# A graph-attention layer whose projection uses seven half-height products per pair, and one early sum made by VectorE

## The chip, the core and the metric

The kernel runs on one core of a Trainium2 chip. A core has TensorE (PE, with its weight loads shown apart as PEld), VectorE (DVE), ScalarE (ACT), GpSimd (POOL) and SyncE (SP), each with its own instruction queue; semaphores order them against each other. Data lie in SBUF, matmul results in PSUM, which has eight banks of 128 x 512 float32. The metric is the device time of one execution in microseconds. The kernel before took 1846.09 us, the median of three runs (1845.35, 1846.09, 1849.65).

## What is computed

Two layers over a graph of 4096 nodes with 512 float32 features each. Each layer normalizes its input, takes the positive part, and adds the layer's output to the input.

```python
# layer 0: a graph convolution with the dense matrix
rowsum = adj.sum(axis=1)
d = where(rowsum > 0, rowsum ** (-0.5), 0.0)
x = x + relu((d[:, None] * adj * d[None, :]) @ h @ W0 + b)      # h = relu(layernorm(x))
# layer 1: attention over the entries of adj that are above 0
e = leaky_relu(Wh1 + Wh2.T, 0.2)                                # Wh = h @ W, times two halves of a
p = softmax(where(adj > 0, e, -1e12), axis=1)
n = -softmax(where(adj > 0, -e, -1e12), axis=1)
x = x + elu(concatenate([p @ h, n @ h], axis=1) @ wtrans)       # wtrans is 1024 x 512
```

About 0.8% of the matrix is above 0 (an entry is drawn with 1/256, then made symmetric), so layer 1 needs only few rows of h for each block of nodes.

## The kernel before, in words

**Layer 0** (to about 960 us) is a dense product in which blocks of the matrix are added on VectorE before they are multiplied (L1105). Meanwhile it finds, for every 128 rows, which columns occur, and writes the new h, with the attention scores and a mask of bytes, to tables in DRAM.

**Layer 1** works on blocks of 64 nodes; two blocks are a pair, which owns 128 rows of the output. A pair's needed rows of h are fetched by 21 indirect DMAs on GpSimd (`gather`, L506; 8, 6 and 7 of them for the parts a = 0, 1, 2), each bringing 128 rows, and one plain load on SP (`load_own`) for the pair's own rows. Every part has two buffers (`g_pools[k % 2, a]`), used in turn. An even block uses parts 0 and 1 (15 slots of 128 rows), an odd one parts 1 and 2 (14 slots).

For a block r there are these steps:

- `weights(r)` (L1756-1791), for each of the two parts: ScalarE copies the gathered scores into a PSUM bank (e, L1765), VectorE adds the block's own scores (z, L527), ScalarE scales (L1768), VectorE takes the maximum (L1769), ScalarE forms exp of z and of -z (L1773), VectorE masks both into p (L1777). At the end one VectorE reduction over the slots gives the sums (`total`, L1787). z and e take a PSUM bank each.
- `product(r)`: one matmul of `total` with ones (cs, L580), then the matmuls of p with the gathered rows (u, L556). Here p has 64 columns a slot, 32 nodes times two signs, and the two halves of a block stand side by side on TensorE, in columns 0-63 and 64-127. VectorE inverts the sums (L585, L588) and ScalarE scales u (us, L1815).
- `turn(r)`: four transposes of us on TensorE (tp, L595) and two ScalarE copies (ut, L602), one for each sign, into the pair's `uts`.
- The pair's projection: `project1(j, 0)` and `project1(j, 1)`, four matmuls of 128 x 512 each (L1826) into one bank; the second is part of `finish1`, which then applies elu, adds x1 and stores (L1843-1848). The profile counts two passes for a float32 matmul, so a half is eight instructions there.

The order on each engine is written out by the loop over `order`, 62 blocks: at step k come product(k); the gathers for the pair two ahead, part 0 at even k, parts 1 and 2 at odd k; weights(k + 2); turn(k - 1); then the first half of a projection at odd k, or finish1 at even k. Queues are in order, so an instruction that waits holds up what stands behind it on its engine. A gather waits until the last matmul that reads its buffer is done. PSUM banks are given out in turn from one pool of eight (`bank`), so a new tile waits for the tile eight allocations before it.

The last pair is treated apart (`finish_last`, L1856-1873, two column halves of 256, matmuls L1860).

**The early pair.** Pair 16, blocks 33 and then 32, is done inside the end of layer 0, because layer 0 leaves its last two tiles of h (`late_h`) for the end: `early_pair` (L1496) gathers its rows ahead, makes weights and products while layer 0 finishes, and adds the late rows (`late_weights0`, `late_product0`) when they exist. Its sums are matmuls with one column: one for every slot, 14 for block 33 and 15 for block 32 (`sum0`, L1541), and then the late ones, which end the same accumulation.

Of the kernel before, what the change touches and what calls it, by code (L numbers as in the profile page):

```python
# [273 lines left out]
def gcn_gat_kernel(  # L274
# [54 lines left out]
    ps = ctx.enter_context(tc.tile_pool(name="ps", bufs=8, space=PSUM))  # L329
    dram = ctx.enter_context(tc.tile_pool(name="dram", bufs=1, space=DRAM))  # L330

    def bank(name):
        return ps.tile([P, 512], F32, tag="ps", name=name)
# [257 lines left out]
    def turn_u(r, u, ut, pin=False):  # L591

        tp = ps.tile([P, FC, 2, 2, SB], F32, tag="ps", name=f"tp{r}")
        for c in range(FC):
            i = nc.tensor.transpose(  # L595
                tp[:, c].rearrange("p h g i -> p (h g i)"), u[:, c * P : (c + 1) * P], ident
            )
# [7 lines left out]
    late_mask = ctx.enter_context(sbuf(name="late_mask", bufs=1, side="right"))  # L605
    late_m = late_mask.tile([P, EJ, TT * P], U8, name="late_m")
    with sbuf(name="y0", bufs=1) as y_pool, sbuf(name="wa", bufs=1) as wa_pool, sbuf(name="bits", bufs=4) as bits_pool, sbuf(name="small0", bufs=4) as small, ExitStack() as rest, ExitStack() as lists:
# [104 lines left out]
        def sum_counts(g):  # L712
            o_ps = places[g] = ps.tile([NH, NE + 1, NK + 1], F32, tag="ps", name=f"o_ps{g}")
# [782 lines left out]
        def early_pair(work, at_pool, prod, rows):  # L1496

            late = ctx.enter_context(sbuf(name="late", bufs=1, side="right"))
# [38 lines left out]
            def sum0(r, ks):  # L1537
                if r not in sums0:
                    sums0[r] = bank(f"cs{r}")
                for k in ks:  # L1540
                    nc.tensor.matmul(  # L1541
                        sums0[r][:, 0:1],
                        ps0[r][:, k].rearrange("p h g i -> p (h g i)"),
                        ones[:, 0:1],
                        start=k == 0,
                        stop=k + 1 == slots0(r) + n_late,
                    )

# [63 lines left out]
            mask0(first)  # L1612
            product0(first)
# [13 lines left out]
            for r in (first, second):  # L1627
                sum0(r, range(slots0(r)))
# [62 lines left out]
    def sparse_layer1():  # L1691
        nonlocal verdict
        with ExitStack() as pools:
# [60 lines left out]
            def weights(r):  # L1754
# [6 lines left out]
                for gt, k, n in parts(r):  # L1761
# [3 lines left out]
                    nc.scalar.copy(e[:, :, 0:1], t)  # L1765
                    scores(s, z, e[:, :, 0:1])
# [50 lines left out]
            def turn(r):  # L1817
                if r % 2 == 0:
                    uts[r // 2] = ut_pool.tile([P, 2, FC, P], F32, tag="ut", name=f"ut{r // 2}")
                turn_u(r, us.pop(r), uts[r // 2])  # L1820
# [14 lines left out]

            def finish1(j):
                x1 = work.tile([P, F], F32, tag="x1", name=f"x1_{j}")
                nc.sync.dma_start(out=x1, in_=x1_dram[j])
                project1(j, 1)
                del uts[j]  # L1840
                po = halves.pop(j)
# [3 lines left out]
                y = work.tile([P, F], F32, tag="y", name=f"y1_{j}", bufs=1)  # L1845
# [4 lines left out]

            def finish_last(j):

                e = work.tile([P, F], F32, tag="eo", name=f"eo{j}", bufs=1)
                y = work.tile([P, F], F32, tag="y", name=f"y1_{j}", bufs=1)
                for h in range(2):
                    cols = slice(h * H, (h + 1) * H)  # L1856
                    po = bank(f"o1_{j}_{h}")[:, :H]
                    for g in range(2):
                        for c in range(FC):
# [3 lines left out]
                                wts[g][:, c, cols],  # L1863
# [7 lines left out]
                    nc.vector.scalar_tensor_tensor(yh, po, 0.0, last_x1[:, cols], ALU.max, ALU.add)  # L1871
# [7 lines left out]
            lates, halves = {}, {}  # L1879
# [23 lines left out]
            for k, r in enumerate(order):  # L1903
# [11 lines left out]
                if k + 2 < len(order):  # L1915
                    weights(order[k + 2])
                    if wanted and order[k + 2] % 8 == 7:
                        load_s(wanted.pop(0))
                if k:
                    turn(order[k - 1])  # L1920
# [13 lines left out]
                if k % 2 and k > 1:  # L1934
                    project1(order[k - 3] // 2, 0)
                elif k > 2:
                    finish1(order[k - 4] // 2)
            last_x1 = work.tile([P, F], F32, tag="x1", name="x1_last")
            nc.sync.dma_start(out=last_x1, in_=x1_dram[order[-1] // 2])
# [45 lines left out]
```

## Time and profile before

| what | us |
|---|---|
| median of three runs | 1846.09 |
| the profiled execution | 1844.97 |
| its span, first to last instruction | 1843.2 |
| PE / DVE / ACT / POOL busy | 1825.7 / 1332.2 / 674.4 / 821.7 |
| u products, L556, 2604 instructions | 572.4 |
| projections, L1826, 496 instructions | 223.2 |
| sums over slots, L1787, 62 instructions | 209.1 |
| gathers of layer 1, L506, 672 instructions | 637.5 |
| early sums, L1541, 66 matmuls from 982.6 to 997.0 | 250 ns median each |

Times of instructions on TensorE overlap: matmuls are pipelined, and a following one starts before the last has drained, so the mean of an instruction is longer than the distance from one to the next. For what a group costs, the distance between starts, or a stretch of the chain of waits, is read. GpSimd's busy time covers the work on a DMA's descriptors, not the transfer, and what lies between two gathers shows as idle time. In a row of the costliest groups the columns are busy time, mean duration in ns of one, and the idle time before them with what ended it. In a row of stretches the columns are the stretch, its length, the busy times (with counts) of PE, PEld, DVE, ACT and POOL, then the granted TensorE clock, the share of the DMA engines and GB/s.

### The profile page before, as it was taken

How to read it: one execution, taken by the hardware profiler on the slowest of the kernel's cores; microseconds unless marked ns; L12 is line 12 of the kernel's file. 1: busy time of each engine (PE TensorE's matmuls, PEld its weight loads, DVE VectorE, ACT ScalarE, POOL GpSimd, SP SyncE). 2: the span in 40 equal slices, each digit the busy share in tenths (PEclk: the TensorE clock that was granted, in tenths of full speed). 3: DMA queues.
4: the chain of work that ended last, by engine and by line, in shares of the span. 5: the costliest groups of instructions: out<-in, count | busy, mean ns of one | idle time of the engine just before them, and what ended most of it. 6: DMA issues, size and time to landing. Idle time of an engine off the chain costs nothing.

```text
span 1843.2 us, 23672 instructions
## 1 busy us (share of the span) xinstructions
PE 1825.7 (99%) x7708; PEld 1035.6 (56%) x7708; DVE 1332.2 (72%) x2882; ACT 674.4 (37%) x1390; POOL 821.7 (45%) x919
## 2 busy tenths in 40 slices
PE   8999999999999999999999999999999999999998
PEld 3444448888888888888744333333333333333333
DVE  6766669799988999897536777677666767676671
ACT  6777762322122412122223333333333333333331
POOL 3101000003432132433067777777777777777740
PEclk9999999999999999999999999999999999999999
DMA  9999975848684859494799999999899988988860
GB/s 370 402 335 333 338 250 184 276 143 280 193 276 151 271 176 289 139 285 148 230 329 350 318 303 311 335 310 343 287 350 301 331 296 298 303 288 289 297 208 25
DMA packets 217212, 504.28 MB, mean 274 GB/s; under 512 B 35059, under 2 KB 69395, under 8 KB 217078
## 3 DMA queue, kind: packets, MB, share of 16 engines
q0 software_dynamic: 62560, 233.71, 37.6%
q1 hardware_dynamic: 108864, 225.92, 36.1%
q10 hardware_dynamic: 45654, 43.04, 7.3%
q8 instruction: 63, 1.03, 0.2%
q14 instruction: 71, 0.58, 0.1%
HBM read 457.77 MB, written 103.45 MB: 304 GB/s over the span
## 4 chain that ended last, share of the span: by engine, by line
PE 96%; DMA 2%; DVE 1%; issue 0%; ACT 0%; ACTq 0%; DVEq 0%; SPq 0%
PE p L1105 33%; PE u L556 32%; PE o L1826 12%; PE acc L1064 5%; PE yp L890 5%; PE q L1465 3%; PE tp L595 2%; DMA ar<-in_adj 2%; PE counts L867 1%; PE tx L831 1%; PE cs L1541 0%; PE cs L580 0%; PE o L1860 0%; DVE key L429 0%; DVE lst L427 0%; DMA w_sb<-in_w 0%
## 5 line engine op out<-in xcount | busy, mean ns | idle before, releaser
L506 POOL DMA_INDIRECT g<-table,idx x672 | 637.5, 949 | 277.9 <-issue 172.1
L556 PE MATMUL u<-g,p 128*64 128x512 f32 x2604 | 572.4, 595 | 0.0
L556 PEld LDWEIGHTS u<-g,p 128*64 128x64 f32 x2604 | 181.6, 137 | 338.8 <-issue 318.7
L442 POOL DMA_INDIRECT ld<-lst,off x160 | 144.5, 903 | 339.4 <-DMA ld<-lst,off 148.8
L1105 PE MATMUL p<-y,at 128*128 128x256 f32 x832 | 248.0, 380 | 0.0
L1105 PE MATMUL p<-y,sums 128*128 128x256 f32 x832 | 247.4, 379 | 0.0
L1105 PE MATMUL p<-t,sums 128*128 128x256 f32 x832 | 245.3, 379 | 0.0
L1826 PE MATMUL o<-wt,ut 128*128 128x512 f32 x496 | 223.2, 593 | 0.0
L1787 DVE TENSOR_REDUCE total<-p 128x128 f32<-128x1920 f32 (+1 forms) x62 | 209.1, 3372 | 2.0
L1105 PEld LDWEIGHTS p<-t,sums 128*128 128x128 f32 x832 | 158.1, 190 | 21.6 <-issue 0.2
L1105 PEld LDWEIGHTS p<-y,at 128*128 128x128 f32 x832 | 157.2, 190 | 23.1 <-issue 2.2
L1105 PEld LDWEIGHTS p<-y,sums 128*128 128x128 f32 x832 | 158.1, 190 | 21.4
L527 DVE TENSOR_TENSOR z<-e,s 128x512 f32<-128x512 f32 (+1 forms) x112 | 71.3, 637 | 102.4 <-ACT e L1765 102.4
L1826 PEld LDWEIGHTS o<-wt,ut 128*128 128x128 f32 x496 | 89.5, 190 | 89.6 <-issue 89.4
L852 ACT ACTIVATE junk<-ar 128x1024 bf16<-128x1024 f32 x128 | 134.6, 1051 | 8.1 <-DMA ar<-in_adj 5.7
L930 ACT ACTIVATE m<-at 128x1024 uint8<-128x1024 f32 x110 | 113.0, 1047 | 51.9 <-DVE t_all L1032 16.1
L1105 PE MATMUL p<-t,at 128*128 128x256 f32 x416 | 123.9, 380 | 1.2 <-DVE w L975 1.2
L890 PE MATMUL yp<-w_sb,hx_t 128*128 128x512 f32 x256 | 119.0, 609 | 1.2 <-DVE hx_t L836 1.2
L1064 PE MATMUL acc<-y,at 128*128 128x512 f32 x256 | 120.2, 594 | 0.0
L427 DVE MAX8 lst<-key 128x8 f32<-128x488 f32 (+13 forms) x154 | 95.0, 617 | 3.4
L1765 ACT COPY e<-g 128x8 f32<-128x8 f32 (+1 forms) x124 | 22.2, 181 | 203.2 <-DMA g<-table,idx 199.3
L1777 DVE SCALAR_TENSOR_TENSOR p<-g,e 128x512 f32<-128x512 uint8 (+1 forms) x124 | 78.9, 637 | 23.2 <-ACT e L1773 20.1
(221 smaller groups left out, 2006.9 us busy)
## 6 DMA issues: line engine op xcount, KB each, us to landing
ar<-in_adj SPq DMA_DIRECT2D x128, 512.0 KB, 6.9
at<-in_adj_t SPq DMA_DIRECT2D x112, 512.0 KB, 4.8
table<-table SPq DMA_DIRECT2D x45, 1032.0 KB, 8.5
table<-m ACTq DMA_DIRECT2D x48, 256.0 KB, 8.9
g<-table,idx POOLq DMA_INDIRECT x672, 5.0
g<-table SPq DMA_DIRECT2D x32, 322.0 KB, 4.8
at<-in_adj_t SPq DMA_DIRECT2D x32, 256.0 KB, 6.7
xr<-in_x SPq DMA_DIRECT2D x32, 256.0 KB, 5.0
```

Source lines behind the costliest of these rows:

```text
L427: nc.vector.max(top, key)
L442: return nc.gpsimd.indirect_dma_start(out=lst_dram[g][e % TURNS][:, :], out_offset=bass.IndirectOffsetOnAxis(ap=off[g][:, e, c : c + 1], a ...
L506: i = nc.gpsimd.indirect_dma_start(out=gt[:, k, :], out_offset=None, in_=table[2 * n // RPT], in_offset=bass.IndirectOffsetOnAxis(ap=idx[n ...
L556: i = nc.tensor.matmul(u[h * RB : (h + 1) * RB], p[:, k, h].rearrange("p g i -> p (g i)"), row(k), start=begin and k == HALVES[r % 2][h][0 ...
L852: nc.scalar.activation(junk, ar, AF.Identity, accum_out=parts[j][:, c : c + 1])
L890: nc.tensor.matmul(yp, hx_t[j][:, c * P : (c + 1) * P], w0_sb[:, c, :], start=c == 0, stop=c == FC - 1,)
L930: nc.scalar.activation(m, at, AF.Sign)
L1064: nc.tensor.matmul(a, at[:, 0, it * P : (it + 1) * P], y0[j], start=j == 0, stop=j == NJ - 1)
L1105: i = nc.tensor.matmul(out, left[:, x * P : (x + 1) * P], right, start=jp == 0 and first, stop=jp == NP - 1 and (final or not first),)
L1777: nc.vector.scalar_tensor_tensor(p[:, k : k + n, :, g], mask.rearrange(four, h=2), 0.0, x.rearrange(four, h=2), ALU.is_gt, ALU.mult,)
L1787: nc.vector.tensor_reduce(total, q, AX.X, ALU.add)
L1826: i = nc.tensor.matmul(halves[j], uts[j][:, g, c, :], wts[g][:, c, :], start=g == 0 and c == 0, stop=g == 1 and c == FC - 1,)
```

## The change

It has two parts.

The early pair: after block 33's masks, one VectorE reduction over its 14 slots puts the sums into a corner of `ut0` (`sum_first`), and one matmul with ones takes the place of the 14 (`begin_sum`). Block 32 keeps its 15.

Layer 1's projection, for the pairs 2 to 29 of the 31 in `order`, becomes a product of 2 x 2 blocks by seven products instead of eight. The left matrix of a pair has 64-row blocks a11, a21 (the positive sign, even and odd block of nodes) and a12, a22 (the negative sign); the right one, `wtrans`, has blocks b of 512 x 256. Sums of blocks are made first: of `wtrans` once (`sum_wtrans`, four VectorE operations of 128 x 1024, at k = 6), of the turned u per pair (`sum_ut`, four of 128 x 256 with tp read from PSUM). Each product is 64 rows by 256 columns by four chunks of 128. Two of them stand side by side on TensorE, columns 0-63 and 64-127. Part 0 (at odd k) holds four products, 16 matmuls; part 1 (in `finish1`) three, where the third is split by its chunks over the two sides, 12 matmuls. They end in two PSUM banks, `left` and `right`, with a bank each of their own; the other banks become six in place of eight from k = 6. `join_blocks1` puts the output together: four ScalarE copies and five VectorE operations.

With that go:

- the odd blocks' scores are made by 14 ScalarE activations of 128 x 64 (7 a part) into z, in place of a ScalarE copy and a VectorE addition a part;
- `finish1` stands ahead of `turn` at even k from 6 on, and elu's minimum reads SBUF, not PSUM;
- b12's place in `wts[0]` holds a difference, so b12 is loaded again from DRAM for the last pair (`load_again`, an SP load into a gather buffer), and the last pair's x1 load stands in `finish_last`;
- the early pair's right-side pools are closed at k = 6, which makes room for the sums.

```diff
-    ps = ctx.enter_context(tc.tile_pool(name="ps", bufs=8, space=PSUM))
+    psum = ctx.enter_context(ExitStack())
+    ps = {}
+    def new_banks(name, n, own=()):
+        psum.close()
+        for tag in (*own, "ps"):
+            bufs = n if tag == "ps" else 1
+            pool = tc.tile_pool(name=f"{name}{tag}", bufs=bufs, space=PSUM, reuse_waits="tile")
+            ps[tag] = psum.enter_context(pool)
+    new_banks("all", 8)
...
+            def sum_first():
+                total = ut0[:, 0, 0, :]
+                q = ps0[first][:, : slots0(first)].rearrange("p k h g i -> p (h g i) k")
+                nc.vector.tensor_reduce(total, q, AX.X, ALU.add)
+                return total
+            def begin_sum(r, total):
+                sums0[r] = bank(f"cs{r}")
+                nc.tensor.matmul(sums0[r][:, 0:1], total, ones[:, 0:1], start=True, stop=False)
...
             begin_weights0(first)
             mask0(first)
+            total = sum_first()
             product0(first)
...
             late_weights0(first)
             late_weights0(second)
-            for r in (first, second):
-                sum0(r, range(slots0(r)))
+            begin_sum(first, total)
+            sum0(second, range(slots0(second)))
...
-                    nc.scalar.copy(e[:, :, 0:1], t)
-                    scores(s, z, e[:, :, 0:1])
+                    if r % 2 and "left" in ps:
+                        for c in range(n):
+                            nc.scalar.activation(z[:, c], s, AF.Identity, bias=t[:, c])
+                    else:
+                        nc.scalar.copy(e[:, :, 0:1], t)
+                        scores(s, z, e[:, :, 0:1])
...
-                turn_u(r, us.pop(r), uts[r // 2])
+                tp = turn_u(r, us.pop(r), uts[r // 2])
+                if r % 2 and blocked and r != order[-1]:
+                    sum_ut(r // 2, tp)
...
+            def sum_wtrans():
+                new_banks("few", 6, ("left", "right"))
+                early.close()
+                pool = pools.enter_context(sbuf(name="blocks", bufs=1, side="right"))
+                blocked["t"] = t = pool.tile([P, 3, FC, H], F32, name="wt_sums")
+                blocked["s"] = pool.tile([P, 4, FC, RB], F32, name="ut_sums")
+                blocked["k"] = pool.tile([P, H], F32, name="shared")
+                b11, b12 = wts[0][:, :, :H], wts[0][:, :, H:]
+                b21, b22 = wts[1][:, :, :H], wts[1][:, :, H:]
+                op = nc.vector.tensor_tensor
+                op(t[:, 0], b22, b12, ALU.subtract)
+                op(b12, b12, b11, ALU.subtract)
+                op(t[:, 1], b22, b12, ALU.subtract)
+                op(t[:, 2], b21, t[:, 1], ALU.subtract)
+            def sum_ut(j, tp):
+                def four(t):
+                    return t.rearrange("p c (h i) -> p c h i", h=2)
+                (a11, _), (a12, a22) = [
+                    [four(uts[j][:, g, :, x * RB : (x + 1) * RB]) for x in range(2)]
+                    for g in range(2)
+                ]
+                b21, b22 = tp[:, :, :, 0, :], tp[:, :, :, 1, :]
+                s = [four(blocked["s"][:, n]) for n in range(4)]
+                op = nc.vector.tensor_tensor
+                op(s[2], a11, b21, ALU.subtract)
+                op(s[1], b22, s[2], ALU.subtract)
+                op(s[0], b21, a22, ALU.add)
+                op(s[3], a12, s[1], ALU.subtract)
+            def multiply_blocks1(j, part):
+                s, t = blocked["s"], blocked["t"]
+                if part == 0:
+                    blocks[j] = [
+                        ps[tag].tile([P, 512], F32, tag=tag, name=f"{tag}{j}")
+                        for tag in ("left", "right")
+                    ]
+                bx, by = blocks[j]
+                (a11, _), (a12, a22) = [
+                    [uts[j][:, g, :, x * RB : (x + 1) * RB] for x in range(2)] for g in range(2)
+                ]
+                b11, b21, b22 = wts[0][:, :, :H], wts[1][:, :, :H], wts[1][:, :, H:]
+                top, low = slice(0, RB), slice(RB, P)
+                left, right = slice(0, H), slice(H, F)
+                half = FC // 2
+                todo = (
+                    (
+                        ((bx, top, left, a11, b11), (bx, low, left, a22, t[:, 2])),
+                        ((by, top, left, a12, b21), (by, low, left, s[:, 2], t[:, 0])),
+                    ),
+                    (
+                        ((bx, top, right, s[:, 3], b22), (bx, low, right, s[:, 0], wts[0][:, :, H:])),
+                        (
+                            (by, top, right, s[:, 1, :half], t[:, 1, :half]),
+                            (by, low, right, s[:, 1, half:], t[:, 1, half:]),
+                        ),
+                    ),
+                )[part]
+                for pair in todo:
+                    for c in range(pair[0][3].shape[1]):
+                        for out_ps, rows, cols, a, b in pair:
+                            i = nc.tensor.matmul(
+                                out_ps[rows, cols],
+                                a[:, c],
+                                b[:, c],
+                                start=part == 0 and c == 0,
+                                stop=part == 1 and c == a.shape[1] - 1,
+                            )
+                            tc.keep_in_program_order(i)
+            def join_blocks1(j, q):
+                multiply_blocks1(j, 1)
+                bx, by = blocks.pop(j)
+                k, op = blocked["k"], nc.vector.tensor_tensor
+                nc.scalar.copy(k[:RB], by[RB:, H:])
+                nc.scalar.copy(q[:RB, H:], bx[RB:, H:])
+                nc.scalar.copy(q[:RB, :H], by[:RB, :H])
+                op(k[:RB], by[:RB, H:], k[:RB], ALU.add)
+                op(k[:RB], bx[:RB, :H], k[:RB], ALU.add)
+                nc.scalar.copy(k[RB:], k[:RB])
+                op(q[:RB, H:], q[:RB, H:], k[:RB], ALU.add)
+                two = [RB, 2, H]
+                op(
+                    q[RB:].rearrange("p (a f) -> p a f", a=2),
+                    by[RB:, :H].unsqueeze(1).to_broadcast(two),
+                    k[RB:].unsqueeze(1).to_broadcast(two),
+                    ALU.add,
+                )
+                op(q, bx, q, ALU.add)
+                return q
...
-                project1(j, 1)
+                y = work.tile([P, F], F32, tag="y", name=f"y1_{j}", bufs=1)
+                if j in blocks:
+                    po = join_blocks1(j, y)
+                else:
+                    project1(j, 1)
+                    po = halves.pop(j)
                 del uts[j]
-                po = halves.pop(j)
                 e = work.tile([P, F], F32, tag="eo", name=f"eo{j}", bufs=1)
                 nc.vector.tensor_scalar(e, po, 0.0, None, ALU.min)
                 nc.scalar.activation(e, e, AF.Exp)
-                y = work.tile([P, F], F32, tag="y", name=f"y1_{j}", bufs=1)
                 nc.vector.scalar_tensor_tensor(y, po, 0.0, x1, ALU.max, ALU.add)
...
+            def load_again():
+                t = g_pools[1, 0].tile([P, CHUNKS[0], ROW], I32, tag="g", name="wt_again")
+                b = t.bitcast(F32)[:, :FC, :H]
+                nc.sync.dma_start(out=b, in_=wtrans[:F, H:].rearrange("(c p) f -> p c f", p=P))
+                return b
...
-                                wts[g][:, c, cols],
+                                wts[g][:, c, cols] if g or not h else b12[:, c],
...
+                if k > 5 and k % 2 == 0:
+                    finish1(order[k - 4] // 2)
+                if k == 6:
+                    sum_wtrans()
                 if k:
                     turn(order[k - 1])
...
-                    project1(order[k - 3] // 2, 0)
-                elif k > 2:
-                    finish1(order[k - 4] // 2)
-            last_x1 = work.tile([P, F], F32, tag="x1", name="x1_last")
-            nc.sync.dma_start(out=last_x1, in_=x1_dram[order[-1] // 2])
+                    if k > 6:
+                        multiply_blocks1(order[k - 3] // 2, 0)
+                    else:
+                        project1(order[k - 3] // 2, 0)
+                elif k == 4:
+                    finish1(order[0] // 2)
+                if k + 2 == len(order):
+                    b12 = load_again()
             finish1(order[-3] // 2)
```

More of the change, by code (lines that the diff above doesn't have):

```diff
@@ L328, in gcn_gat_kernel @@
     const = ctx.enter_context(sbuf(name="const", bufs=1))
-    ps = ctx.enter_context(tc.tile_pool(name="ps", bufs=8, space=PSUM))
+    psum = ctx.enter_context(ExitStack())
[7 more added lines that the diff above has]
+    new_banks("all", 8)
     dram = ctx.enter_context(tc.tile_pool(name="dram", bufs=1, space=DRAM))
     def bank(name):
-        return ps.tile([P, 512], F32, tag="ps", name=name)
+        return ps["ps"].tile([P, 512], F32, tag="ps", name=name)
     ones = const.tile([P, P], F32, name="ones")
@@ L591, in turn_u @@
     def turn_u(r, u, ut, pin=False):
-        tp = ps.tile([P, FC, 2, 2, SB], F32, tag="ps", name=f"tp{r}")
+        tp = ps["ps"].tile([P, FC, 2, 2, SB], F32, tag="ps", name=f"tp{r}")
         for c in range(FC):
@@ L602, in turn_u @@
             nc.scalar.copy(half.rearrange("p c (h i) -> p c h i", h=2), tp[:, :, :, g, :])
-    late_mask = ctx.enter_context(sbuf(name="late_mask", bufs=1, side="right"))
+        return tp
+    early = ctx.enter_context(ExitStack())
+    late_mask = early.enter_context(sbuf(name="late_mask", bufs=1, side="right"))
     late_m = late_mask.tile([P, EJ, TT * P], U8, name="late_m")
@@ L712, in sum_counts @@
         def sum_counts(g):
-            o_ps = places[g] = ps.tile([NH, NE + 1, NK + 1], F32, tag="ps", name=f"o_ps{g}")
+            o_ps = places[g] = ps["ps"].tile([NH, NE + 1, NK + 1], F32, tag="ps", name=f"o_ps{g}")
             for e in range(NE + 1):
@@ L1496, in early_pair @@
         def early_pair(work, at_pool, prod, rows):
-            late = ctx.enter_context(sbuf(name="late", bufs=1, side="right"))
+            late = early.enter_context(sbuf(name="late", bufs=1, side="right"))
             late_h = late.tile([P, n_late, ROW_W], F32, name="late_h")
@@ L1848, in finish1 @@
                 nc.sync.dma_start(out=out[j * P : (j + 1) * P, :], in_=e)
+            def load_again():
[3 more added lines that the diff above has]
+                return b
             def finish_last(j):
+                x1 = work.tile([P, F], F32, tag="x1", name=f"x1_{j}")
+                nc.sync.dma_start(out=x1, in_=x1_dram[j])
                 e = work.tile([P, F], F32, tag="eo", name=f"eo{j}", bufs=1)
@@ L1870, in finish_last @@
                     nc.scalar.activation(eh, eh, AF.Exp)
-                    nc.vector.scalar_tensor_tensor(yh, po, 0.0, last_x1[:, cols], ALU.max, ALU.add)
+                    nc.vector.scalar_tensor_tensor(yh, po, 0.0, x1[:, cols], ALU.max, ALU.add)
                     nc.vector.scalar_tensor_tensor(eh, eh, -1.0, yh, ALU.add, ALU.add)
@@ L1878, in sparse_layer1 @@
             with_late = (2 * pairs[0], 2 * pairs[0] + 1)
-            lates, halves = {}, {}
+            lates, halves, blocks, blocked = {}, {}, {}, {}
             order = [r for n in pairs for r in (2 * n, 2 * n + 1)]
```

## The prediction

> **What bounds the kernel now.** I read the page's busy shares, then the chain of work that ended last in the sparse layer, then what GpSimd waited for, and last the timelines around the end of the gathers and around the early pair.
>
> ```profile
> PE 1825.7 (99%) x7708; PEld 1035.6 (56%) x7708; DVE 1332.2 (72%) x2882; ACT 674.4 (37%) x1390; POOL 821.7 (45%) x919
> L442 POOL DMA_INDIRECT ld<-lst,off x160 | 144.5, 903 | 339.4 <-DMA ld<-lst,off 148.8
> L1105 PE MATMUL p<-y,at 128*128 128x256 f32 x832 | 248.0, 380 | 0.0
> ```
>
> TensorE is busy for 99% of the span: a cut on it is worth its full length until another engine is late. The chain in layer 1 (start, duration, work):
>
> ```profile
> 1341.08 0.59 PE tp L595 x4
> 1341.67 3.44 PE o L1826 x8
> 1345.10 0.12 PE cs L580 x2
> 1345.22 8.73 PE u L556 x40
> 1353.95 0.59 PE tp L595 x4
> 1354.54 3.44 PE o L1826 x8
> 1357.97 0.12 PE cs L580 x2
> 1358.09 9.59 PE u L556 x44
> 1367.68 0.59 PE tp L595 x4
> ```
>
> Two blocks, a pair, take 1367.68 - 1341.08 = 26.60 us on PE without a gap; 6.88 of it is the projection (two runs of eight passes of 128x512, 0.43 each). GpSimd is nearly as full, though its busy share hides it:
>
> ```profile
> 1653.03 1.20 POOL L506 DMA_INDIRECT g<-table,idx  x1 [0.30 <-issue]
> 1763.85 0.94 POOL L506 DMA_INDIRECT g<-table,idx  x1 [0.65 <-PE u L556]
> 1765.10 0.94 POOL L506 DMA_INDIRECT g<-table,idx  x1 [0.30 <-issue]
> 1778.85 0.95 POOL L506 DMA_INDIRECT g<-table,idx  x1 [0.30 <-issue]
> ```
>
> A gather is 0.95 busy and 0.30 between, 1.25 in all; 21 per pair are 26.25 us, against PE's 26.60. The gathers begin at 964.76 and run without a free moment to 1178; from there, once a pair, one waits 0.65 instead of 0.30 for the u product to free its buffer. Those 23 waits hold 8.35 us above the 0.30: all that GpSimd could save if PE freed every buffer at once.
>
> The last rows to read are where the gathers meet PE at their end (one row each of ACT, DVE, PE):
>
> ```profile
> 1774.69 0.17 ACT L1765 COPY e<-g 128x7 f32<-128x7 f32 x1 [6.34 <-DMA g<-table,idx]
> 1777.38 0.68 DVE L1777 SCALAR_TENSOR_TENSOR p<-g,z 128x512 f32<-128x512 uint8 x1
> 1783.94 2.37 PE L556 MATMUL u<-g,p 128*64 128x512 f32 x10
> ```
>
> The ACT copy starts when the gather of the last even block's second part has landed. VectorE's queue holds that part's scores in front of the masks of the first part, which end at 1778.06. The order of the tiles through PSUM lets the u product of the block before (here 1783.94) begin only when these masks have released their banks, so a late gather stops PE two blocks earlier than its own product. The slack is 1783.94 - 1778.06 = 5.9 us.
>
> **The projection on PE.** Seven products of 64 rows and four chunks, two passes each, two products side by side: 28 pairs of 256-column passes instead of 16 passes of 512. No row has 64x256 passes side by side. From below: the L1105 passes of 128x256 follow each other at 0.216 (364 in 78.56 us) and u's side-by-side passes of 64x512 at 0.4285, the same as one full pass, so 28 x 0.215 = 6.02. From above: the two weight loads of 0.137 (PEld row of L556), if they ran one after the other, 0.274 a pair, 7.67. In u the two loads start 5 ns apart, so I take 0.215: -0.86 a pair. Moving from 128-wide to two 64-wide halves and back costs about 0.15 and 0.05 where u meets tp and cs; part 0 adds one such round trip a pair, +0.2. Net -0.66, for 28 pairs -18.5.
>
> **The early pair.** 58 records of L1541 stand in 982.60-990.40, 0.134 each. 28 of the first block's become 2, so 26 x 0.134 = -3.5 on PE. This is the one place of low clock (PEclk is the column after PE to POOL; the two last are DMA share and GB/s):
>
> ```profile
> 982.00:986.00 4.00, 4.00 (x35) 3.41 (x31) 3.75 (x8) 3.10 (x7) 3.08 (x4) 1.00 1.02 398
> 986.00:990.00 4.00, 4.00 (x28) 4.00 (x28) 4.00 (x3) 0.54 (x1) 2.97 (x4) 0.72 1.04 401
> 990.00:994.00 4.00, 4.00 (x11) 1.15 (x10) 1.93 (x5) 1.51 (x4) 2.90 (x4) 0.50 1.00 375
> ```
>
> The late_h product of one block takes 3.61 there and that of the next 1.87; with fewer one-column products up to 1.7 more may return. The price is one reduction on VectorE, 3.27 (the L1787 row of 128x1792), where it is busy 17.6 of 22 us before 982. If all of it delays the late weights (ready at 978.1), PE loses about as much as it gains. So A is between 0 and -5.2 on PE; I take -3.5.
>
> **Where this runs out.** PE could gain 18.5 + 3.5 = 22.0. But the gathers' start at 964.76 is not touched, so at the last gate PE can be early by 5.9 + 8.35 = 14.2 and no more. From some pair on, PE waits for gathers and A adds nothing. After the gate there is little: the last two projections save 0.86 twice at part 1, against 0.4 for two switches and about 1.4 for the join behind part 1, which holds the single y and eo buffers: +0.1.
>
> **What it adds beside PE.** VectorE gets 4 sums of u, 5 joins, and loses 2 score operations; 18.8 us a pair (226.2 in 320) become about 22.3. ACT goes from 9.6 (115.95 in 320) to about 14: fourteen 128x64 activations and four copies. Both fit in 26, but the chain from the gate to the odd block's masks is about 12.1 of 14 us: 2 us cover it. Layer 1's one-time sums (four of 128x1024) are about 4.4 on VectorE, covered by the same slack once or twice. finish1 moves ahead of the turn: its passes now run before the four transposes, its x1 load, join and store are issued 0.59 (tp) earlier, and on ACT its four copies (0.38 each by the 128x256 ut copies, L602) stand ahead of the odd block's ut copies. What is late then is sum_ut and part 0, but that is a whole u product (8.73) away. SP reloads a block of weights once, off the chain, and the moved x1 load has over 10 us.
>
> **What it does to GpSimd.** In layer 0 the 55 L442 gathers that start while a VectorE operation with two SBUF inputs runs take 1.023, the others 0.840. In layer 1 the one at 1653.03 took 1.20 beside the 0.68 of eo L1847 that had 0.38 left: the gather waits for the rest less 0.13. Before, L1847 is the only long one and its end mostly falls just after a start: gathers average 0.949 against 0.946, 0.06 a pair. After there are five: two sums of 0.42, the y of 0.68, the eo sum of 0.68 and an eo minimum of about 0.41 from SBUF to SBUF. With starts at random against a pitch of 1.25, the sum of (d - 0.13) squared over 2.5 is 0.34 a pair; if none meets, 0; if each meets a start in full, 1.96. By L1847's own row, five such would be 0.2. I take 0.25: 25 pairs before the last gathers, 6.3, and 1.2 for the one-time sums, 7.5 us. The Trainium skill, "SBUF — State Buffer", section "Who interferes with whom", says that an operation with two SBUF inputs stops GpSimd only where that reads SBUF, and supposes that descriptor generation needs only the write side. By that supposition only the eo minimum would cost, 0.03 a pair, an estimate of some 13 us gain in all; the L442 rows speak against it.
>
> **Sum.** -14.2 + 7.5 + 0.1 = -6.6 on the profiled execution of 1844.97 (span 1843.2 and 1.8 around it): 1838.3. The median shown is 1846.09, 1.1 above: 1839.4.
>
> **Rivals.**
> - The gathers keep their pitch and nothing meets (locked starts, as L1847 now): -14, 1832.
> - The bound from GpSimd doesn't hold, because PE alone decides: -22 to -24, about 1823. For it only the 1.25 pitch would have to shrink; no row shows a shorter one.
> - Slower side, contention: from 0.52 a pair on ((14.1 - 1.2) / 25) GpSimd eats the gain, and at 0.8 it is +7, 1853. For it: six more VectorE operations a pair that may take the port, and GpSimd now never idle, so no loss is made good. Against: the 0.34 of random starts.
> - The 64x256 passes are limited by weight loads: +0.8 instead of -0.86, with the switch +1.0 a pair, +28 - 3.5: 1870. Against it are the 5 ns in u.
> - Six PSUM banks: product k's sums wait for the masks of k+1, on VectorE behind joins and sums. Over 2 us more on that chain and PE waits at each pair; 0.3 a pair from there gives up 8: 1847.
>
> **How the numbers follow.** Within 0.3% (5.5 us) no change can be told. GpSimd-bound with 0.02 to 0.5 a pair 0.50 (1833-1845; faster 0.32, same 0.18); nothing meets 0.13, faster; PE alone 0.07, faster; contention over 0.5 0.14 (half same, half slower); weight loads 0.10, slower; the banks 0.06 (half same, half slower). Faster 0.52, same 0.28, slower 0.20. The range 1827 to 1852 leaves out PE alone, weight loads and the far end of contention, under 0.2; the likeliest alone is 1833 to 1845.
>
> **What will show it.** Period of the chain: 26.25 to 26.5 with PE gaps in front of u or cs that end on VectorE's masks, not 25.95 without a gap. GpSimd's 0.65 waits gone, gathers above 0.95 beside the new VectorE operations, last gather about 1778.85 - 1 instead of 8 earlier. Side-by-side passes at 0.215. L1541 over by about 986. A part-1 run of passes that starts later than tp ends, gaps that end on ACT, or passes at 0.27 would prove it wrong.

## The result and the profile after

The changed kernel takes 1844.45 us, the median of 22 runs (1841.12 to 1846.62); the kernel before, in runs beside them, 1847.77 (1844.56 to 1851.47). The ratio is 0.9986, 95% interval 0.9981 to 0.9992: 0.14%, 2.6 us by the ratio and 3.3 by the medians, less than half of the 6.7 that were forecast. The interval leaves out 1, but the change lies within the 0.3% below which the prediction calls it no change. The two profiled executions differ even less: 1844.97 before, 1844.78 after (spans 1843.2 and 1842.9).

The page of the changed kernel, its span, busy times and costliest groups (columns as before):

```profile
span 1842.9 us, 26588 instructions
PE 1815.9 (99%) x8802; PEld 1059.4 (57%) x8802; DVE 1405.9 (76%) x3085; ACT 821.6 (45%) x1826; POOL 832.7 (45%) x919
L516 POOL DMA_INDIRECT g<-table,idx x672 | 649.5, 966 | 270.9 <-issue 181.9
```

PE is busy for 10 us less than before, and the span is the same. The gathers (now L516) take 966 ns on average instead of 949. The chain of waits, in a stretch of layer 1 where nothing stalls:

```profile
1491.14 0.86 PE right L1929 x8
1492.00 0.59 PE tp L605 x4
1492.59 0.12 PE cs L590 x2
1492.71 9.59 PE u L566 x44
1502.30 0.59 PE tp L605 x4
1502.89 1.88 PE left L1929 x16
1504.76 1.73 PE right L1929 x16
1506.49 0.31 PE cs L590 x2
1506.80 8.73 PE u L566 x40
1515.54 1.73 PE left L1929 x16
1517.26 0.86 PE right L1929 x8
1518.13 0.59 PE tp L605 x4
```

A pair takes 1518.13 - 1492.00 = 26.13 us of PE work, 0.48 less than 26.60. But PE doesn't always get to do it without a pause. What PE waited for:

```profile
PE cs L590 <- DVE p L1804: 5.8, 4, 2.1
PE tp L605 <- DVE p L1804: 1.6, 1, 1.6
PE u L566 <- DVE p L1804: 1.0, 6, 0.2
```

These waits did not exist before. They end on VectorE's masks, and the masks wait for a gather to land. The end of the gathers in the changed kernel (rows of POOL, ACT, DVE and PE; the first is the last gather of the last even block's second part):

```profile
1774.31 0.95 POOL L516 DMA_INDIRECT g<-table,idx  x1 [0.30 <-issue]
1780.26 0.18 ACT L1792 COPY e<-g 128x7 f32<-128x7 f32 x1 [6.34 <-DMA g<-table,idx]
1782.95 0.68 DVE L1804 SCALAR_TENSOR_TENSOR p<-g,z 128x512 f32<-128x512 uint8 x1
1783.69 0.65 PE L566 MATMUL u<-g,p 128*64 128x512 f32 x2 [0.15 <-DVE p L1804]
```

The u product that began at 1783.94 before begins at 1783.69, at once after the masks: the slack of 5.9 us is gone, and so is PE's gain. The last gather of all starts at 1783.06, 4.2 us later than before (1778.85), although the 0.65 waits, one a pair, are gone (one wait of 1.29 is left). One piece of why, on POOL and on DVE at the same time:

```profile
1525.21 1.12 POOL L516 DMA_INDIRECT g<-table,idx  x1 [0.30 <-issue]
1526.63 1.43 POOL L516 DMA_INDIRECT g<-table,idx  x1 [0.30 <-issue]
1525.09 0.42 DVE L1896 TENSOR_TENSOR ut_sums<-ut,ut_sums 128x256 f32<-128x256 f32 x1
1526.56 0.68 DVE L1974 SCALAR_TENSOR_TENSOR eo<-eo,y 128x512 f32<-128x512 f32 x1
```

Two gathers start inside two VectorE operations that read SBUF twice, and end 0.17 and 0.48 late. In layer 1's records from 1000 us on, the gathers sort like this ("inside" are those that start with more than 0.1 us of such an operation still to run, "outside" all others):

| kernel | inside: count, mean us | outside: count, mean us | sum of all above 0.9455 each, us |
|---|---|---|---|
| before | 2, 1.10 | 615, 0.946 | 0.3 |
| changed | 45, 1.191 | 572, 0.946 | 11.4 |

Of the 45, 36 take over 0.99 us. In each of these 36 the excess over 0.9455 is what was left of the operation when the gather started, less 0.12 to 0.13 us. So the excess follows from the operation's end, and isn't only found beside it.

### The profile page after: what moved, and what is told of

Same layout as the page of the kernel before. It is cut to its first block, busy times and chain, and to the rows that moved or that the text cites. A ratio compares the mean times of both kernels' runs of the same rounds, so it can differ in the third digit from the quotient of the medians.

```text
span 1842.9 us, 26588 instructions
## 1 busy us (share of the span) xinstructions
PE 1815.9 (99%) x8802; PEld 1059.4 (57%) x8802; DVE 1405.9 (76%) x3085; ACT 821.6 (45%) x1826; POOL 832.7 (45%) x919
## 4 chain that ended last, share of the span: by engine, by line
PE 76%; DMA 7%; POOL 7%; DVE 5%; issue 3%; ACT 1%; ACTq 0%; DVEq 0%; POOLq 0%; SPq 0%
PE p L1117 33%; PE u L566 19%; POOL g L516 7%; PE acc L1076 5%; PE yp L902 5%; DMA g<-table,idx 5%; PE q L1477 3%; PE left L1929 3%; PE right L1929 2%; DMA ar<-in_adj 2%; DVE total L1814 1%; PE tp L605 1%; DVE p L1804 1%; PE counts L879 1%; PE tx L843 1%
## 5 line engine op out<-in xcount | busy, mean ns | idle before, releaser
L516 POOL DMA_INDIRECT g<-table,idx x672 | 649.5, 966 | 270.9 <-issue 181.9
L1796 DVE TENSOR_TENSOR z<-z,y 128x512 f32<-128x512 f32 (+1 forms) x124 | 79.6, 644 | 63.5 <-ACT y L1795 63.0
L1790 ACT ACTIVATE z<-s,g 128x64 f32<-128x64 f32 x378 | 120.0, 317 | 9.7
L1792 ACT COPY e<-g 128x8 f32<-128x8 f32 (+1 forms) x70 | 12.8, 184 | 206.4 <-DMA g<-table,idx 190.3
L812 ACT ACTIVATE rrb<-rrb 128x1 f32<-128x1 f32 x32 | 6.5, 203 | 214.4 <-DVE rrb L811 212.2
L537 DVE TENSOR_TENSOR z<-e,s 128x448 f32<-128x448 f32 (+1 forms) x58 | 37.9, 654 | 80.6 <-ACT e L1792 80.6
```

The source lines that it names most:

```text
L516: i = nc.gpsimd.indirect_dma_start(out=gt[:, k, :], out_offset=None, in_=table[2 * n // RPT], in_offset=bass.IndirectOffsetOnAxis(ap=idx[n ...
L1790: nc.scalar.activation(z[:, c], s, AF.Identity, bias=t[:, c])
```

## Experiments

Six questions were asked: what each part does alone, whether gathers set the end, whether the operations with two SBUF inputs lengthen them, what the one-time sums cost, where executions of the same kernel differ, and whether the parts' gains add.

### Each part alone

The kernel before with the early sum alone:

```diff
             mask0(first)
+            total = sum_first()
             product0(first)
...
-            for r in (first, second):
-                sum0(r, range(slots0(r)))
+            begin_sum(first, total)
+            sum0(second, range(slots0(second)))
```

> The kernel before with the early pair's first block summed by VectorE, and nothing of the projection. Theory (the gathers on GpSimd set the end once PE is early by more than their slack): PE reaches the first u product of layer 1 about 1.8 us earlier, as in the changed kernel (995.36 against 997.20), and with the kernel before's 5.9 us of slack at the last gate all of it stays: 1.8 us faster than before, the two late_h products both at the low clock (3.6 and 3.5). Rival (the early gain is eaten at the early pair itself, by VectorE's 3.3 us in front of the late weights): within 0.3 us of before, the first u product at 997.

Measured: 1842.89 us against 1847.57 of the kernel before, ratio 0.9974 (0.9966 to 0.9983), more than expected. The first u product of layer 1 starts at 996.00, a lead of 1.2 where 1.8 was expected, and all of it is still there at the last gate (1782.73 against 1783.94), as expected. Why the runs show more than the two profiles is seen below (the profiles of before).

The changed kernel without the early sum (those lines the other way round):

> The changed kernel with the early pair's 14 sum matmuls as before, so the projection's change alone. Theory: GpSimd's row of gathers sets the end, so PE's 1.8 us of the early pair are worth nothing here: the time of the changed kernel within 1 us, the last gather at 1783 as there, PE stalls shorter by about 1.8 in all. Rival (PE sets the end, and its waits are only local): 1.8 us slower than the changed kernel.

Measured: 1845.89 us, ratio 0.9993 (0.9982 to 1.0003), 1.4 us above the changed kernel, between the two expectations; the intervals overlap, so the times don't choose. The last gather was expected at 1783 and starts at 1780.55 in the profile, where the lengthening is 10.1 instead of 11.4. Alone, the parts bring 4.7 and 1.7 us by the medians (the 1.7 not clear of zero); together 3.3. The gains don't add: the early sum alone is no slower than the whole change (0.9974 against 0.9986).

### Fewer gathers

Two of a pair's 21 gathers become SP loads of the same size.

```diff
-        for k in range(LISTED[a]):
+        for k in range(LISTED[a] - (2 if pin and a == 2 else 0)):
...
+                if a == 2:
+                    for k2 in (5, 6):
+                        r0 = n // EJ * ER + (n % EJ // 2 * 2 + k2 - 5) * P
+                        nc.sync.dma_start(out=gt[:, k2, :], in_=table[2 * n // RPT][r0 : r0 + P, :])
```

> The changed kernel with 2 of a pair's 21 gathers replaced by SP loads of the same size from neighbouring rows (the two slots then hold rows that were not asked for). Theory: 19 gathers take 23.8 us a pair, PE never waits for them after the first pairs, and the period is PE's own 26.12: 28 times 0.48 and the early 1.8, less the stall at the one-time sums, 12 to 14 us faster than before. Rival (six banks or VectorE's chain stop PE whatever the gathers do): the stalls of 1 to 2.7 us before the sums matmul stay, and the time stays near the changed kernel's.

Measured: 1832.96 us, ratio 0.992 (0.9905 to 0.9936), 14.6 us faster than before and in the span 13.0 (1830.2 against 1843.2). The period is 26.12 in nearly every pair, and no wait of PE on masks over 0.2 us is left. Six banks and VectorE's longer chain are as in the changed kernel, and so is the length of a gather (963 ns on average), so what stopped PE was their number. The same edit in the kernel before:

> The control of the run with 19 gathers: the kernel before with the same 2 gathers a pair replaced by SP loads of the same size (rows that were not asked for). Theory: PE was the bound there and never waited for a gather after the first pairs, so its period stays 26.60 and the time is that of the kernel before within 2 us, apart from the early pair, where the loads also change what the DMA queues carry (there the run with the seven products gained up to 3 us by a clock that did not fall). Rival (gathers held the kernel before too): 5 us faster or more.

Measured: 1846.61 against 1846.42, ratio 0.9999 (0.9987 to 1.0012), period 26.60. There PE was the bound.

### The join in PSUM

The joined output, its minimum and its exponential stay in the banks left and right, so that in the join only one input of each operation is in SBUF. The result is the same.

```diff
-                op(k[:RB], by[:RB, H:], k[:RB], ALU.add)
-                op(k[:RB], bx[:RB, :H], k[:RB], ALU.add)
-                nc.scalar.copy(k[RB:], k[:RB])
-                op(q[:RB, H:], q[:RB, H:], k[:RB], ALU.add)
+                kp = by[:RB, H:]
+                op(k[:RB], kp, k[:RB], ALU.add)
+                op(kp, bx[:RB, :H], k[:RB], ALU.add)
+                nc.scalar.copy(k[RB:], kp)
+                op(q[:RB, H:], q[:RB, H:], kp, ALU.add)
...
-                op(q, bx, q, ALU.add)
-                return q
+                op(bx, bx, q, ALU.add)
+                return bx, by
...
-                nc.vector.tensor_scalar(e, po, 0.0, None, ALU.min)
-                nc.scalar.activation(e, e, AF.Exp)
+                nc.vector.tensor_scalar(ep, po, 0.0, None, ALU.min)
+                nc.scalar.activation(ep, ep, AF.Exp)
                 nc.vector.scalar_tensor_tensor(y, po, 0.0, x1, ALU.max, ALU.add)
-                nc.vector.scalar_tensor_tensor(e, e, -1.0, y, ALU.add, ALU.add)
+                nc.vector.scalar_tensor_tensor(e, ep, -1.0, y, ALU.add, ALU.add)
```

> The changed kernel with the joined output, its minimum and its exponential kept in PSUM, so that of VectorE's per-pair operations only the last of the sums of u still reads two inputs from SBUF. Theory (a gather that starts during such an operation waits for its end): the lengthening of the layer-1 gathers falls from 11.1 us over the kernel before to about 3 (2.2 of the one-time sums, under 0.05 a pair), the last gather starts 6 to 8 us earlier, at about 1776, and the time falls by 5 to 8 us against the changed kernel. Rival 1 (the lengthening comes from DMA traffic): gathers stay at 0.966 on average and the time within 1 us. Rival 2 (PE waits for the six banks and VectorE's longer chain, not for gathers): gathers get shorter and the time stays.

Measured: 1837.38 us, ratio 0.9951 (0.9937 to 0.9964): 10.2 us faster than before and some 6.5 faster than the changed kernel (0.9951 against 0.9986). Its busy times and its gathers, from its page:

```profile
span 1835.5 us, 26536 instructions
PE 1813.8 (99%) x8802; PEld 1060.0 (58%) x8802; DVE 1414.9 (77%) x3085; ACT 815.6 (44%) x1826; POOL 824.1 (45%) x919
L516 POOL DMA_INDIRECT g<-table,idx x672 | 640.5, 953 | 271.1 <-issue 181.5
```

VectorE is busier than in the changed kernel (1414.9 against 1405.9) and yet the gathers are shorter, 953 against 966 ns. Inside an operation with two SBUF inputs (counted as in the table) start 13 (mean 1.243), outside 604 (0.945); the sum above 0.9455 is 3.8 instead of 11.4, and the last gather starts at 1774.6 instead of 1783.06. From 1292 on PE runs at 26.12 a pair but for one of 26.44. Rivals 1 and 2 both fall: moving inputs to PSUM moved no DMA, and the time followed the gathers.

### The one-time sums

```diff
-                op(t[:, 0], b22, b12, ALU.subtract)
-                op(b12, b12, b11, ALU.subtract)
-                op(t[:, 1], b22, b12, ALU.subtract)
-                op(t[:, 2], b21, t[:, 1], ALU.subtract)
+                nc.sync.dma_start(out=t[:, 0], in_=wtrans[F:, H:].rearrange("(c p) f -> p c f", p=P))
+                nc.sync.dma_start(out=t[:, 1], in_=wtrans[F:, :H].rearrange("(c p) f -> p c f", p=P))
+                nc.sync.dma_start(out=t[:, 2], in_=wtrans[:F, H:].rearrange("(c p) f -> p c f", p=P))
```

> The changed kernel without the four one-time sums of wtrans on VectorE: their three places are loaded with blocks of wtrans by SP instead, and the output is not the reference's. Theory: the 2.2 us by which gathers are lengthened at 1063-1092 and PE's stall of 1.9 in front of the transposes at 1089 both go, and with them the stall and the low-clock stretch of 4 us that follow at 1117-1131. The gathers still set the end, so 2 to 3 us faster than the changed kernel, no more. Rival (the one-time sums are hidden by the gathers' slack there): within 1 us.

Measured: 1842.76 us, ratio 0.9981 (0.9972 to 0.9991). By the medians that is 1.7 below the changed kernel, by the ratios 0.9, and the intervals overlap: the times don't choose between theory and rival. The lengthening before 1092 falls from 2.5 to 0.5 us, about the 2.2 expected (the whole from 11.4 to 9.0), and the slow u product at 1119.8 is gone. The stall in front of the transposes is not: there it is 2.79 us, against 1.64 in the changed kernel. But it ends on something else. The copy of the scores that the masks wait for waits itself for the own rows' load on SP, which stands among the three loads of 512 KB that the edit adds:

```profile
1069.57 0.43 SPq L1876 DMA_DIRECT2D wt_sums<-in_wtrans  x1
1070.04 0.60 SPq L1877 DMA_DIRECT2D wt_sums<-in_wtrans  x1
1070.96 1.18 SPq L530 DMA_DIRECT2D g<-table  x1
1087.10 0.17 ACT L1792 COPY e<-g 128x7 f32<-128x7 f32 x1 [7.53 <-DMA g<-table]
```

In the changed kernel that load was issued at 1070.39 and landed 6.75 us later, and one of the sums (L1878) stands with 1.12 us in the chain of waits to the masks. So the run shows that the sums lengthen the gathers there; whether the stall of 1.64 came from them it doesn't show.

### Where executions of the kernel before differ

The kernel before, unchanged, was profiled twice more.

> The kernel before, unchanged, for a second profile. What is asked: where executions of the same kernel differ. If the low clock at the early pair is what differs, the second late_h product takes 3.6 (as in the run of the projection alone) or 1.87 (as in the profile shown), the first u product of layer 1 starts at 998.7 or 997.2, and the whole differs by the same 1.5 to 2 us, since PE has no gap behind it. If the difference lies elsewhere, the periods of layer 1 or the start of the early pair differ instead.

> A third profile of the kernel before, for the same question.

Measured: spans 1846.8 and 1843.8. PE in the first of them, around the early sums and the late products:

```profile
984.77 10.18 PE L1541 MATMUL cs<-ones,p_pair 128*128 128x1 f32 x58
994.88 3.27 PE L556 MATMUL u<-late_h,p_pair 128*64 128x512 f32 x8
998.62 1.94 PE L556 MATMUL u<-late_h,p_pair 128*64 128x512 f32 x8
1001.03 2.37 PE L556 MATMUL u<-g,p 128*64 128x512 f32 x10
```

and in the profile that the prediction used:

```profile
982.60 7.87 PE L1541 MATMUL cs<-ones,p_pair 128*128 128x1 f32 x58
990.40 3.68 PE L556 MATMUL u<-late_h,p_pair 128*64 128x512 f32 x8
994.80 1.94 PE L556 MATMUL u<-late_h,p_pair 128*64 128x512 f32 x8
997.20 2.37 PE L556 MATMUL u<-g,p 128*64 128x512 f32 x10
```

The same 58 records take 7.87 or 10.18 us, by where the low clock falls. From the early pair's last long run of u (964.42, 966.59, 963.51) to layer 1's first u product it is 32.8, 34.4 and 34.4 us in the three profiles; with the early sum on VectorE 31.5 in the changed kernel and in the run of it alone. So the profile that I worked from was a quick one there, by 1.6. Against the other two the early sum is worth 2.9, just under the 3.1 to 6.3 that the runs of it alone give. Later profiles spread more: over the six profiles with the early sum that stretch is 27.7 to 31.5, over the six without it 32.8 to 35.8 (the runs at 2050 and above left out), and the means, 30.1 and 34.1, are 4.0 apart. The rest of what differs lies in the opening of layer 0, which ends at 272.4, 274.6 and 271.4; from the first u product on, all three have the same periods to 0.03 us.

### Do the gains add once gathers no longer set the end?

The join in PSUM without the early sum.

> The output joined in PSUM without the early sum on VectorE, where the kernel before runs at about 1847. Theory: 1.5 to 3.5 us slower than the run with the output joined in PSUM (0.9951 of the kernel before), so 0.996 to 0.997 of it, since PE is the bound over most of layer 1 there. Rival (the gathers still set the end): within 1 us, 0.995.

Measured: 1839.69 us, ratio 0.9954 (0.994 to 0.9969), against 0.9951 (0.9937 to 0.9964) with the early sum. The ratios are as the rival says, but with five runs each the intervals are too wide to choose, and the medians are 2.3 apart. The profiles do choose. PE's cs and first u at the last gate, without and with the early sum:

```profile
1775.63 0.28 PE L590 MATMUL cs<-ones,total 128*128 128x1 f32 x2
1775.84 1.51 PE L566 MATMUL u<-g,p 128*64 128x512 f32 x6
...
1775.61 0.28 PE L590 MATMUL cs<-ones,total 128*128 128x1 f32 x2
1775.82 1.51 PE L566 MATMUL u<-g,p 128*64 128x512 f32 x6
```

The first u product of layer 1 starts at 997.89 without the early sum and at 995.56 with it; at the last gate these 2.3 us are gone, and both spans are 1835.5. So the rival's mechanism holds in the profiles. In both, PE catches up with the gathers early in layer 1 and waits for masks last at about 1278; what it had been ahead is lost there, and the same PE work follows. The gathers run back to back from 984 until then, so PE's place at 1278 is theirs.

### More operations with two SBUF inputs

```diff
+                if po is y:
+                    for _ in range(2):
+                        nc.vector.scalar_tensor_tensor(y, po, 0.0, x1, ALU.max, ALU.add)
                 nc.vector.scalar_tensor_tensor(y, po, 0.0, x1, ALU.max, ALU.add)
```

> The kernel with two extra operations a pair that read SBUF twice, where the kernel before runs at about 1847. Theory: the lengthening after 1092 goes from 8.9 to about 15 and the time is 4 to 7 us above the changed kernel, 1849 to 1851. Rival (only VectorE's length counts, and it has slack): within 2 us of the changed kernel.

Measured: 1845.73 us, ratio 0.9989 (0.9977 to 1.0001), by the medians 1.3 above the changed kernel, intervals overlapping: the theory's 4 to 7 us missed, and the time is what the rival expected. The lengthening after 1092 is 10.7, not 15. By the count of the table, 46 gathers start inside such operations, against 45 without the extra ones; 37 are lengthened. In the changed kernel the sum of eo (L1974) and the y (L1973) make 6.4 of the lengthening after 1092; here the two extra operations in front of them make 6.9, and these two only 0.3. So the cause of a single lengthened gather stands, but how many are hit can't be got from random starts: extra operations in a row with the old ones take over their hits and hardly add any.

### Runs that decide nothing

In two sets of runs the kernel before itself took 2049 and 2048 us. The profiles of the other kernels there show PE stopped for 87 to 123 us in front of u products, and no cause was found. The same two extra operations with one input from PSUM (first edit, against the run with SBUF inputs), and the one-time sums in halves on top of the join in PSUM (second edit, two of four operations shown), ran only there.

```diff
-                        nc.vector.scalar_tensor_tensor(y, po, 0.0, x1, ALU.max, ALU.add)
+                        nc.vector.scalar_tensor_tensor(y, left, 0.0, x1, ALU.max, ALU.add)
```

> The same two extra operations a pair, of the same size, but with one input from PSUM (the bank left), the output wrong as well. Theory: the lengthening stays at about 9 and the time within 2 us of the changed kernel, though VectorE is as busy as in the other run. Rival (VectorE's chain): as slow as the run with SBUF inputs.

```diff
+                for x in (slice(0, 2), slice(2, 4)):
+                    op(t[:, 0, x], b22[:, x], b12[:, x], ALU.subtract)
...
+                    op(t[:, 2, x], b21[:, x], t[:, 1, x], ALU.subtract)
```

> The output joined in PSUM, and the four one-time sums of wtrans split in eight halves of 128x512, interleaved as before. Theory: the longest stretch that a gather can wait for halves, so the lengthening at 1063-1092 falls from about 2.4 to 1 or 1.5; PE's early stalls shrink by as much; 0.5 to 2 us faster than the run with whole sums. Rival: PE is the bound there already, within 0.5 us.

Measured there, in the first set: two extra operations from SBUF 2063.97 (1.0074 of the kernel before), from PSUM 2102.93 (1.0249), join in PSUM without the early sum 2131.69 (1.0403), with halves 2130.44 (1.039). In the second set the first three again, 1.0065, 1.0268 and 1.041, and the join in PSUM 1.0405. So under what slowed these runs the join in PSUM was 4% slower than the kernel before, for a reason that stays open; its gain is shown only where the kernel before takes about 1847. One thing holds here as well: gathers that start inside an operation with two SBUF inputs (counted as in the table) take 1.15 to 1.48 on average, the others 0.945 to 0.949. Open are the extra operations' price by place of input, and the halves.

## Why the prediction was right and where it went wrong

**The bound moves to GpSimd: right.** The 0.65 waits went, PE got gaps that end on VectorE's masks, and with 19 gathers a pair the gaps and 12 us of time went too. The rivals "PE alone", "weight loads" and "the six banks" fall with that run and with the passes at 0.216.

**PE's gain per pair: smaller than forecast, without effect at the gate.** Side-by-side passes of 64x256 follow each other at 1.73 / 8 = 0.216, as forecast. The round trip through the column halves costs more than 0.2: part 0 takes 3.60 instead of 3.44, and the cs behind it 0.31 instead of 0.12. So -0.48, not -0.66.

**The slack of 14.2: nearly right, 13.1.** At the last gate 5.88 were used up, and the waits of GpSimd shrank by 7.25 instead of 8.35.

**The step that fails is the term of VectorE's operations, "I take 0.25", 7.5 us in all.** The mechanism is right and the size is not: it measured 11.0 (11.4 less the 0.3 of before), 8.7 over 25 pairs, 0.35 a pair, and 2.3 around the one-time sums instead of 1.2. The prediction went below the 0.34 of random starts because L1847 hits almost nothing in the kernel before. It even set that too high: its 0.06 a pair is from a mean over all 672 gathers, in which 1.8 of the 2.1 us of lengthening lie before 1000 us; L1847 makes 0.01 a pair. But that it hits so little rests on two engines being in step. From 1204 on, each pair's gathers restart on a release by u, and of the 21 ends of L1847 behind it 16 come 0.04 to 0.09 us after a gather's start, too late to hold it:

```profile
1759.13 0.68 DVE L1847 SCALAR_TENSOR_TENSOR eo<-eo,y 128x512 f32<-128x512 f32 x1
1759.75 0.95 POOL L506 DMA_INDIRECT g<-table,idx  x1 [0.30 <-issue]
```

Before there are such waits the distance takes any value, 0.03 to 1.21, and in the third profile of the kernel before four of the six L1847 before 1178 lengthen a gather. In the changed kernel the waits are gone, and the two are out of step. After 1092 the same operation, now L1974, makes 4.7 of the 8.9 us that are lengthened there, y L1973 and the last of the sums of u L1896 1.7 each, the joined corner 0.5, the minimum 0.2. That 0.35 came so near to the 0.34 of random starts is luck: the run of extra operations breaks that rule, and the run without the early sum has 1.3 us less lengthening at the same operations.

**Two things were not in the sum.** The landing: the copy of the last even block starts 5.95 us after its part's last gather, against 4.59 (1780.26 - 1774.31, 1774.69 - 1770.10), 1.4 lost. The row of before:

```profile
1770.10 0.95 POOL L506 DMA_INDIRECT g<-table,idx  x1 [0.31 <-issue]
```

Over the last 26 pairs the median is 5.9 against 4.8 before, and 4.9 with the early sum alone. In the kernels with seven products and 21 gathers it is 5.7 to 6.3; why stays open. And the clock: two stalls were followed by slow u products (granted clock 0.85 over each), of which the second keeps a gather waiting:

```profile
1280.96 0.35 PE L590 MATMUL cs<-ones,total 128*128 128x1 f32 x2 [2.10 <-DVE p L1804]
1281.47 11.31 PE L566 MATMUL u<-g,p 128*64 128x512 f32 x44 [0.15 <-DVE p L1804]
...
1289.63 1.10 POOL L516 DMA_INDIRECT g<-table,idx  x1 [1.29 <-PE u L566]
```

u of 44 records takes 11.3 there and 9.6 elsewhere, and the gather behind it waits 1.29 instead of 0.30: 1.0 of the 1.1 by which the waits shrank less than forecast.

**The ledger of the profiled executions.** Start of the gathers after 983.5: +0.4; their waits -7.25; lengthening +11.0; so the last gather +4.2. With landing +1.4, a remainder of +0.1 and the slack of 5.9, u at the gate is 0.25 earlier, where 6.7 was forecast. The tail is as forecast, within 0.2. The difference of 6.4 is 3.5 of lengthening, 1.4 of landing, 1.1 of waits and 0.4 of the start.

**The base.** I put the median 1.1 above the profiled execution; over 22 runs it is 2.8 above, and 1.6 of the 1.7 is that execution's quick early pair. The kernel before has PE without a gap, so each run's luck there shows in the time; in the changed kernel PE waits for gathers, and much of it shouldn't. The runs fit that (standard deviations of 2.1 and 1.2 us), and it would be why they show 3.3 and the two profiles 0.2; no run tests it by itself.

**The early sum: about right in size on PE (2.9 to 4.0 against 3.5).** That it adds nothing with the other part at the gate fits the profiles (u at the gate 1783.69 with it, 1781.97 without) and isn't settled by the times (1.4 us, intervals overlapping). That it holds even without most of the lengthening, which the two profiles of the join in PSUM show, was not foreseen in the experiment's expectation.

**The page.** The Trainium skill, "SBUF — State Buffer", section "Who interferes with whom", says that an operation with two SBUF inputs contends with a GpSimd instruction that reads SBUF, and infers that descriptor generation is not held by it. Indirect DMAs are held here: those that start inside such operations take 1.191 us, the others 0.946, and 36 of 45 are lengthened. That fits the first, if a gather's reading of its list of offsets counts as such a read. Whether this read is held or the generation of descriptors the traces can't tell; either way a gather is not free of these operations, as one would take it to be from the second.

## What to carry to other kernels

Before paying for PE time in a kernel that gathers, add up the gathers of a stage by their pitch, idle part included: 21 x 1.25 stood 1.3% under PE's period, and that, with the slack at the last gate, was all that any saving on PE could bring. When an engine stops waiting, operations beside it lose their step, so a collision that cost nothing before is no evidence for after; what VectorE reads beside indirect DMAs is best kept to one SBUF input, with the other in PSUM, which gave 6.5 us here at the same result, where the kernel before takes about 1847. Two gains that meet the same bound don't add, so price the second after the first.

## What was not expected of the hardware

The 58 one-column products of the early pair take 7.6 to 10.2 us from run to run, with a granted clock between 0.50 and 1.00 there though PE has no gap, and the low stretch can reach the products behind them (3.6 or 1.87 for the same eight records). After five stalls of PE of 1.2 to 2.1 us the next u product took 11.3 instead of 9.6, at a granted clock of 0.85; after others of 1.0 to 2.8 it did not, so the stall's length alone doesn't tell.
